# Sums of x1 for the values emitted right behind the transposes of x1, ahead of the tanh products of the new pair

## The chip, the cores and the metric

The kernel runs on one core of one Trainium2 chip. The metric is the device time of one execution in microseconds (us). All data are float32, and all matrix products run in float32 on TensorE (PE in the profile). The other engines are VectorE (DVE), ScalarE (ACT), GpSimd (POOL) and SyncE (SP), whose queue issues all of the DMAs that the text speaks of.

## The reference, cut to what matters

Two graph-attention layers follow each other on x of shape (128, 64, 768), each with a residual and a layer norm. The change lies in the stage that computes layer 0 and the values of layer 1.

```python
# layer 0 (12 heads of 64 features)
h    = einsum('bnd,ade->bane', x, W)
th   = tanh(h)
attn = leaky_relu(th @ w_src + swapaxes(th @ w_dst, 2, 3), 0.2)
attn = softmax(where(~adj, -999.0, attn))
feat = elu(attn @ h + b)                  # heads side by side
gate = sigmoid(x @ H_w.T + H_b)
x1   = layernorm(x + gate * feat + (1 - gate) * x)
# layer 1 (6 heads of 128 features)
q, k, v = x1 @ Wq, x1 @ Wk, x1 @ Wv       # biases left out here
out  = layernorm(x1 + softmax(mask(q @ k.T / sqrt(128))) @ v @ Wf + bf)
```

## The kernel before, in words

The 8192 token rows are 64 tiles of 128 rows; two tiles are a pair, so there are 32 pairs. For each pair three products of 256 rows by a 768x768 weight are computed in the first stage (up to about 1530 us of the profile): `h` (the heads), `g` (the gate) and `v` (the values of layer 1, from x1). Each is done in the manner of Strassen and Winograd with seven block products instead of eight, numbered 1 to 7, so `v6` is block product 6 of the values. The operands are sums of blocks. For `v` they are four sums of blocks of x1 transposed (tile `x1T`, written by ScalarE from PE transposes, 768 features by 256 tokens), made on VectorE by `block_sums` into tiles `sv1` to `sv4` (in the profile all are `sv_v`):

```python
        steps = [
            lambda: e.tensor_tensor(s1, a21, a22, ALU.add),        # L240
            lambda: e.tensor_tensor(s2, s1, a11, ALU.subtract),    # L241
            lambda: e2.tensor_tensor(s3, a11, a21, ALU.subtract),  # L242
            lambda: e2.tensor_tensor(s4, a12, s2, ALU.subtract),   # L243
        ]
```

Blocks a11 and a12 are columns of the pair's first tile (called t0 here), a21 and a22 of its second tile (t1). So s1 needs only the transposes of t1, s2 those of both. Products v6, v5, v7 and v3 read s2, s1, s3 and s4.

The stage is a loop over turns p. Turn p computes `h` and `g` for the new pair p, finishes layer 0 of the old pair q = p - 1, and begins its `v`. The order is written out by hand; no scheduler changes it. A list (`TURN`, for turns 2 to 31 of the new pair; `FIRST`, `SECOND` and `LAST` at the ends) gives the block products in order:

```python
TURN = [
    "h1", "h2", "u4", "u3", "h6", "g1", "h5", "h7", "g2", "g6", "h4",
    "h3", "g5", "g7", "v1", "v2", "g4", "v6", "g3", "v5", "v7",
]
```

(`u` is the value product of the turn before.) `step` issues a product on PE and then the PSUM eviction of the product before it. Behind each step come the actions that `was(pos, ...)` (old pair) and `at(pos, new, ...)` (new pair) have put at that position, in the order in which the calls stand in the code. Each engine works through its instructions in that order. `SECOND_OLD` and `LAST_AT` map positions for the second and the last turn.

Names that the prediction uses, for one turn:

- `by_features` at 8 (t1) and 11 (t0): six PE transposes `x1Tp` (L966) and two ScalarE copies (L967) per tile.
- `products` at 11 (n1, the second tile of the new pair) and 12 (n0, the first): ScalarE's tanh of `h` (L888), VectorE's product with the destination weights (L889), GpSimd's product with the source weights (L890).
- `terms` at 13 (n1) and 14 (n0): VectorE's reduction `sd` of both products (L897), a DMA of it to DRAM (`dstd`, L899), and two DMAs that read it back broadcast over the partitions (`dd`, L902).
- `with_bias` at 13 and 14: GpSimd's addition (L913) and two DMAs `hx` (L918, L919).
- `logits` at 16 (n1) and 18 (n0): VectorE's sum of `dd` and `sd` into `att` (L926). Then `leaky` (ScalarE, L936), `masked` (VectorE, L942 to L949), `exps` (ScalarE, L955, writes `prob`).
- In the next turn: the transposes `pTp` of `prob` (L966), the head products `av` (L987), VectorE's `rden` and `fo` (`features`, L1003, L1004), which read `av` from PSUM and free its banks for the next `pTp`; `gate_tanh` on ScalarE (L1067, L1068).
- `x_sums` at 17: the four sums of the next pair's x, on GpSimd (also L240 to L243). In many turns GpSimd also adds blocks of later weights (`wacc`, L366).

VectorE's eviction of `h` is L851, of the gate L866 to L868, of `v` L880.

Of the kernel before, what the change touches and what calls it, by code (L numbers as in the profile page):

```python
# [59 lines left out]
]  # L60
SECOND_AT = {11: 10, 12: 13, 13: 13, 14: 14, 15: 14, 16: 15, 17: 16, 18: 18, 19: 19, 20: 20}
SECOND_OLD = {
    7.5: 12, 0: 7, 1: 7, 2: 8, 3: 9, 4: 10, 5: 11, 6: 12, 7: 12, 8: 13, 9: 14, 11: 15, 12: 15, 15: 16, 16: 17, 19: 19,
}


# [29 lines left out]
    + [f"q{n}" for n in (0, 1, 2, 3, 4, 5, 6, 8, 7, 9, 10, 11, 12)]  # L96
    + ["v1", "v2", "v6", "q13", "v5", "v7", "q14", "v4", "v3"]
)
LAST_AT = {7.5: 8, 3: 3, 4: 4, 5: 5, 6: 6, 7: 7, 8: 9, 9: 10, 11: 12, 12: 13, 15: 15, 16: 17, 19: 18}


PARTS = ("v", "sp", "sc", "ex", "mult", "split", "send", "turn", "join", "cp", "ctx")
# [32 lines left out]
def kernel(  # L135
# [620 lines left out]
    with ExitStack() as ph, ExitStack() as ph_r:  # L756
# [349 lines left out]
        v_sums, carried = {}, {}  # L1106
        summing = sum_weights(sb)
        for p in range(NP + 1):
            q = p - 1
# [6 lines left out]

            turn, of_new, of_old = TURNS.get(p, (TURN, {}, {})) if new else (LAST, {}, LAST_AT)

            def at(pos, ok, *acts, places=of_new):
                if ok:  # L1120
                    plan.setdefault(places.get(pos, int(pos)), []).extend(acts)

            def was(pos, *acts):
                at(pos, old, *acts, places=of_old)

            def do(f, *args):
                return lambda: f(*args)
# [15 lines left out]
            was(7.5, do(gated, t0))  # L1143
            was(8, do(by_features, t1), do(stats, t0))
            was(9, do(normed, t0))
            was(12, do(v_begins))
            was(15, lambda: v_sums[q][0](), lambda: v_sums[q][1](), do(spill_features, q))
            was(16, lambda: v_sums[q][2]())
            was(19, lambda: v_sums[q][3]())

# [4 lines left out]
            at(8, new, do(inputs, p))  # L1155
            at(11, new, do(products, n1))
            was(11, do(by_features, t0))
            at(12, new, do(products, n0))
            at(13, new, do(terms, n1), do(with_bias, n1))
            at(14, new, do(terms, n0), do(with_bias, n0))  # L1160
# [199 lines left out]
```

## Time and profile before

| what | us |
|---|---|
| median of 3 runs (lowest, highest) | 2900.05 (2900.02, 2900.45) |
| the profiled execution, its own time | 2898.46 |
| span of its trace, first to last instruction | 2896.7 |
| PE busy in the span | 2844.1 |
| VectorE busy | 1936.7 |
| GpSimd busy | 1289.3 |
| ScalarE busy | 1061.6 |
| one turn of the stage, where it repeats evenly | 45.61 |

The profile's page gives busy time by engine, the waits view sums for each pair (who waited, for whom) the idle time in us, the number of times and the longest, and the timeline lists instructions by their start in us, their duration in us, engine, line, operation and tiles; in brackets stands the idle time of the engine before it and what ended it. PE's weight loads are listed as an engine of their own, PEld. Between 60 and 1540 us VectorE is busy 1191.07 us of 1480, PE 1457.04.

### The profile page before, as it was taken

The page shows a single profiled execution, that of the slowest core. Times are in us where ns is not written, and L with a number is a line of the kernel's source. Part 1 is how long each engine was busy: PE and PEld are TensorE (multiplying, and loading weights), DVE is VectorE, ACT ScalarE, POOL GpSimd, SP SyncE. Part 2 cuts the span into 40 slices and gives each one's busy share as a digit, 9 for nine tenths or more (in the row PEclk, how much of TensorE's full clock was granted, in tenths as well). Part 3 has the DMA queues.
Part 4 walks back from the last instruction along what each step waited for, and adds up shares of the span by engine and source line. Part 5 has one row for each costly group of instructions (what it writes and reads, how often), then busy time and mean ns, then how long its engine had stood idle before and what let it go on. Part 6 is the DMA issues. An engine that isn't in the chain of part 4 may idle for free.

```text
span 2896.7 us, 47873 instructions
## 1 busy us (share of the span) xinstructions
PE 2844.1 (98%) x18252; PEld 2074.9 (72%) x18252; DVE 1936.7 (67%) x3203; ACT 1061.6 (37%) x1896; POOL 1289.3 (45%) x1253
## 2 busy tenths in 40 slices
PE   7899999999999999999999999999999999999998
PEld 4566556665566655666668888888888888888886
DVE  6888788888878888887874545555545555554556
ACT  2444444444444444444443123333213333322332
POOL 2434454444535444333443454444545443444534
PEclk9999999999999999999999999999999999999999
DMA  5344444544444444333353434432324333223332
GB/s 176 116 154 154 149 136 150 159 142 149 144 154 147 141 141 139 120 122 104 119 203 83 124 101 110 107 91 75 86 82 111 110 101 93 70 84 95 110 88 74
DMA packets 322068, 348.73 MB, mean 120 GB/s; under 512 B 147888, under 2 KB 247216, under 8 KB 321840
## 3 DMA queue, kind: packets, MB, share of 16 engines
q1 hardware_dynamic: 321840, 345.66, 39.1%
q8 instruction: 146, 2.39, 0.4%
q14 instruction: 82, 0.67, 0.1%
HBM read 198.48 MB, written 122.29 MB: 111 GB/s over the span
## 4 chain that ended last, share of the span: by engine, by line
PE 84%; DVE 8%; DMA 3%; ACT 2%; issue 1%; POOL 1%; SPq 1%; POOLq 0%; DVEq 0%; ACTq 0%
PE z_o L494 8%; PE z_k L447 8%; PE z_q L447 8%; PE y_h L270 7%; PE y_v L270 6%; PE y_g L270 6%; PE y_k L447 6%; PE y_o L494 6%; PE y_q L447 5%; PE z_h L270 4%; PE z_v L270 3%; PE z_g L270 3%; PE x_g L270 2%; PE sp L550 2%; PE cp L634 2%; PE x_h L270 2%
## 5 line engine op out<-in xcount | busy, mean ns | idle before, releaser
L574 ACT ACTIVATE sc<-sc 128x512 f32<-128x512 f32 x48 | 30.7, 639 | 615.0 <-DVE sc L571 615.0
L695 POOL TENSOR_TENSOR y<-y,bf_bc 128x768 f32<-128x768 f32 x64 | 114.7, 1815 | 288.3 <-DMA y<-x1d 288.3
L507 DVE TENSOR_TENSOR y<-y,z_o 128x256 f32<-128x256 f32 x320 | 127.5, 418 | 139.6 <-PE z_o L494 139.4
L494 PE MATMUL z_o<-wf,so 128*128 128x256 f32 x896 | 215.8, 383 | 2.3 <-DVE y L507 1.2
L447 PE MATMUL z_q<-xs,w_wq 128*128 128x256 f32 x896 | 213.5, 381 | 0.3 <-POOL xs L411 0.3
L411 POOL TENSOR_TENSOR so<-ctxT 128x256 f32<-128x256 f32 x224 | 160.1, 731 | 92.3 <-PE y_o L494 47.0
L447 PE MATMUL z_k<-xs,hw_wk 128*128 128x256 f32 x840 | 198.5, 379 | 0.0
L1017 POOL TENSOR_TENSOR x<-gate,x 128x768 f32<-128x768 f32 x64 | 118.2, 1848 | 159.6 <-ACT gate L1068 145.3
L494 PEld LDWEIGHTS z_o<-wf,so 128*128 128x128 f32 x896 | 167.2, 190 | 26.9 <-issue 2.0
L447 PEld LDWEIGHTS z_q<-xs,w_wq 128*128 128x128 f32 x896 | 168.7, 190 | 24.3 <-POOL xs L411 0.7
L322 POOL TENSOR_TENSOR rs_b<-ve_b,minus_half 128x1 f32<-128x1 f32 x64 | 40.5, 632 | 312.9 <-DVE ve_b L320 312.1
L890 POOL TENSOR_TENSOR th<-th,wsd 128x768 f32<-128x768 f32 x64 | 117.3, 1832 | 139.8 <-DVE th L889 139.8
L447 PEld LDWEIGHTS z_k<-xs,hw_wk 128*128 128x128 f32 x840 | 159.5, 190 | 21.7
L322 POOL TENSOR_TENSOR rs_a<-ve_a,minus_half 128x1 f32<-128x1 f32 x64 | 36.0, 562 | 307.8 <-DVE ve_a L320 307.8
L411 POOL TENSOR_TENSOR xs<-r,r 128x512 f32<-128x512 f32 x112 | 147.7, 1336 | 39.3 <-DMA r<-x1Td 22.1
L462 DVE TENSOR_TENSOR qT<-qT,z_q 128x512 f32<-128x512 f32 x96 | 66.0, 688 | 141.7 <-PE z_q L447 141.7
L270 PE MATMUL y_v<-wv,sv_v 128*128 128x384 f32 x384 | 136.4, 491 | 9.3 <-DVE sv_v L241 7.5
L270 PE MATMUL y_h<-w_wq,xT 128*128 128x384 f32 x384 | 136.5, 492 | 8.7 <-DMA w_wq<-in_w_dram 8.1
L462 DVE TENSOR_TENSOR kT<-kT,z_k 128x512 f32<-128x512 f32 x96 | 66.1, 688 | 112.3 <-PE z_k L447 111.2
L270 PE MATMUL y_h<-w_wq,sx_x 128*128 128x384 f32 x384 | 136.5, 492 | 4.2 <-ACT h L850 4.2
L270 PE MATMUL y_g<-hw_wk,sx_x 128*128 128x384 f32 x384 | 136.2, 491 | 2.5 <-DVE hw_wk L219 2.2
L270 PE MATMUL z_v<-wv,sv_v 128*128 128x384 f32 x384 | 137.5, 494 | 1.0 <-DVE v L880 1.0
(165 smaller groups left out, 6913.3 us busy)
## 6 DMA issues: line engine op xcount, KB each, us to landing
x<-in_x_dram SPq DMA_DIRECT2D x64, 384.0 KB, 3.6
dd<-dstd SPq DMA_DIRECT2D x128, 192.0 KB, 3.4
x1d<-x SPq DMA_DIRECT2D x64, 384.0 KB, 2.6
x1Td<-x1T SPq DMA_DIRECT2D x32, 768.0 KB, 4.3
vd<-v SPq DMA_DIRECT2D x64, 384.0 KB, 3.1
r<-x1Td SPq DMA_DIRECT2D x96, 256.0 KB, 3.5
v<-vd SPq DMA_DIRECT2D x384, 64.0 KB, 2.3
y<-x1d SPq DMA_DIRECT2D x64, 384.0 KB, 5.4
```

What stands on the lines that cost most here:

```text
L270: T.matmul(to[:, : self.n], lhsT, rhs, start=kc == 0 and not more, stop=kc == HK - 1, skip_group_check=more,)
L322: G.tensor_tensor(rstd, ve, minus_half, ALU.pow)
L411: G.tensor_tensor(t, self.of(x[0]), self.of(x[2]), x[1])
L447: T.matmul(b[:, half * W2 : (half + 1) * W2], w[:, kc, half * P : (half + 1) * P], x[:, kc, :], start=half == kc == 0 and not more, stop=k ...
L462: V.tensor_tensor(at, at, b.rearrange("p (h t) -> p h t", h=2), ALU.add if sign > 0 else ALU.subtract,)
L494: T.matmul(b[:, :W2], x[:, kc, :], w[:, kc, :], start=kc == 0 and not more, stop=kc == 1, skip_group_check=more,)
L507: V.tensor_tensor(at, at, self.banks[path][:, :W2], ALU.add if sign > 0 else ALU.subtract)
L550: T.matmul(self.sp_[gr * N : (gr + 1) * N, (i * 2 + a) * N : (i * 2 + a + 1) * N], qT[:, 2 * self.f + a, at], kT[:, 2 * self.f + a, at], s ...
L634: T.matmul(self.cp_[a][e, at], self.v_[rows, i, gr, e], self.scT_[rows, at], start=True, stop=True,)
L695: G.tensor_tensor(y, y, pools["bf"], ALU.add)
L890: G.tensor_tensor(th[:, 1, :], th[:, 1, :], wsd[:, 1, :], ALU.mult)
L1017: G.tensor_tensor(xp, st[t]["gate"], xp, ALU.mult)
```

## The change

The sums s1 and s2 leave position 15, where they stood behind both reductions `sd`. s1 goes to position 12, ahead of `products` of n0; s2 goes to position 13, ahead of `terms` of n1. s3 (16), s4 (19) and the DMA of x1T (15) stay. The two maps get an entry for position 13, so that in the second turn both sums stand at the mapped position 15 (ahead of the first `logits` that is evaluated there) and in the last turn at 13 and 14.

```diff
 SECOND_OLD = {
-    7.5: 12, 0: 7, 1: 7, ... 11: 15, 12: 15, 15: 16, 16: 17, 19: 19,
+    7.5: 12, 0: 7, 1: 7, ... 11: 15, 12: 15, 13: 15, 15: 16, 16: 17, 19: 19,
 }
-LAST_AT = {7.5: 8, ... 11: 12, 12: 13, 15: 15, 16: 17, 19: 18}
+LAST_AT = {7.5: 8, ... 11: 12, 12: 13, 13: 14, 15: 15, 16: 17, 19: 18}
...
             was(9, do(normed, t0))
-            was(12, do(v_begins))
-            was(15, lambda: v_sums[q][0](), lambda: v_sums[q][1](), do(spill_features, q))
+            was(15, do(spill_features, q))
             was(16, lambda: v_sums[q][2]())
             was(19, lambda: v_sums[q][3]())
...
             at(11, new, do(products, n1))
             was(11, do(by_features, t0))
+
+            was(12, do(v_begins), lambda: v_sums[q][0]())
+            was(13, lambda: v_sums[q][1]())
             at(12, new, do(products, n0))
             at(13, new, do(terms, n1), do(with_bias, n1))
```

In the built programs the instructions of ScalarE, GpSimd and SP's queue are the same and in the same order before and after; PE's too. On VectorE alone two instructions move in each of the 32 old pairs. In most turns its order from the tanh products on becomes:

```
before: th n1, h3 out, th n0,     sd n1, g out, g out, sd n0, s1, s2, v out, s3, att n1
after:  th n1, h3 out, s1, th n0, s2, sd n1, g out, g out, sd n0,    v out, s3, att n1
```

More of the change, by code (lines that the diff above doesn't have):

```diff
@@ L62 @@
 SECOND_OLD = {
-    7.5: 12, 0: 7, 1: 7, 2: 8, 3: 9, 4: 10, 5: 11, 6: 12, 7: 12, 8: 13, 9: 14, 11: 15, 12: 15, 15: 16, 16: 17, 19: 19,
+    7.5: 12, 0: 7, 1: 7, 2: 8, 3: 9, 4: 10, 5: 11, 6: 12, 7: 12, 8: 13, 9: 14, 11: 15, 12: 15, 13: 15, 15: 16, 16: 17, 19: 19,
 }
@@ L98 @@
 )
-LAST_AT = {7.5: 8, 3: 3, 4: 4, 5: 5, 6: 6, 7: 7, 8: 9, 9: 10, 11: 12, 12: 13, 15: 15, 16: 17, 19: 18}
+LAST_AT = {7.5: 8, 3: 3, 4: 4, 5: 5, 6: 6, 7: 7, 8: 9, 9: 10, 11: 12, 12: 13, 13: 14, 15: 15, 16: 17, 19: 18}
 PARTS = ("v", "sp", "sc", "ex", "mult", "split", "send", "turn", "join", "cp", "ctx")
```

## The prediction

> **What bounds the kernel now.** I read the page first, then the waits, then the timeline of a turn that repeats evenly.
>
> ```profile
> span 2896.7 us, 47873 instructions
> PE 2844.1 (98%) x18252; PEld 2074.9 (72%) x18252; DVE 1936.7 (67%) x3203; ACT 1061.6 (37%) x1896; POOL 1289.3 (45%) x1253
> ```
>
> PE is busy nearly all the time, so only what makes PE wait can cost anything. The waits view of PE and of VectorE:
>
> ```profile
> PE y_v L270 <- DVE sv_v L241: 7.5, 9, 1.4
> ...
> DVE th L889 <- ACT th L888: 97.4, 62, 2.6
> DVE h L851 <- ACT h L850: 74.5, 31, 2.7
> ...
> DVE att L926 <- DMA dd<-dstd: 14.5, 9, 4.6
> ```
>
> The first line is what the change can remove: nine times v6 waits for s2, 7.5 us in all (0.26% of the time). But VectorE is no spare engine here. One turn, timeline:
>
> ```profile
> 1235.40 0.96 DVE L889 TENSOR_TENSOR th<-th,wsd 128x768 f32<-128x768 f32 x1 [2.50 <-ACT th L888]
> ...
> 1236.28 0.55 DVE L851 TENSOR_TENSOR h<-z_h,h 128x384 f32<-128x384 f32 x1
> ...
> 1236.44 1.82 POOL L890 TENSOR_TENSOR th<-th,wsd 128x768 f32<-128x768 f32 x1 [4.25 <-DVE th L889]
> ...
> 1237.91 1.17 DVE L889 TENSOR_TENSOR th<-th,wsd 128x768 f32<-128x768 f32 x1 [1.08 <-ACT th L888]
> ...
> 1239.00 1.74 DVE L897 TENSOR_REDUCE sd<-th 128x24 f32<-128x1536 f32 x1
> 1239.15 1.82 POOL L890 TENSOR_TENSOR th<-th,wsd 128x768 f32<-128x768 f32 x1 [0.89 <-DVE th L889]
> ...
> 1243.37 1.31 DVE L240 TENSOR_TENSOR sv_v<-x1T 128x384 f32<-128x384 f32 x1
> ...
> 1244.71 1.23 DVE L241 TENSOR_TENSOR sv_v<-sv_v,x1T 128x384 f32<-128x384 f32 x1
> ...
> 1246.77 1.31 POOL L242 TENSOR_TENSOR sx_x<-xT 128x384 f32<-128x384 f32 x1
> 1247.14 2.24 DVE L926 TENSOR_TENSOR att<-dd,sd 128x768 f32<-128x768 f32 x1
> ...
> 1261.72 0.56 DVE L851 TENSOR_TENSOR h<-x_h,h 128x384 f32<-128x384 f32 x1 [2.47 <-ACT h L850]
> ...
> 1263.11 0.56 DVE L1004 TENSOR_TENSOR fo<-av,rden 128x384 f32<-128x384 f32 x1
> ...
> 1263.78 0.31 PEld L966 LDWEIGHTS pTp<-ident,prob 128*128 128x128 f32 x3 [0.17 <-issue]
> ```
>
> Follow it back from the end. The second half of `pTp` for t0 begins at 1263.78, 0.11 after `fo` has ended (1263.67): it waits for the bank that `fo` frees. `fo` follows an eviction of h, which waits for ScalarE, which runs exps, two gate_tanh and a copy without a gap, and began when VectorE had masked n0; that follows the second `att`, the first `att`, and back to the tanh products. So a chain of VectorE and ScalarE leads from the transposes x1Tp of t0 through `att` of n1 to `pTp` in the next turn. In the timelines of 31 turns, `fo` to PE's next product (the one behind `pTp`) is 0.50 us in 24, and from that product to the next x1Tp of t0 it is 17.20 us in 30. **A turn is 17.20 + 0.50 + the chain.** Where PE arrives later than `fo`, the first x1Tp to that product takes 28.2 us at least; in most turns it is 28.4 to 30.1. These are about 17 us in all, with the 7.5 us among them, since a PE that waits at v6 would otherwise wait at `pTp`. What matters is therefore when `att` of n1 ends, not v6.
>
> **The Trainium skill.** "SBUF — State Buffer", section "Who interferes with whom", says that a VectorE instruction with two SBUF inputs and a GpSimd instruction that reads SBUF exclude each other for the whole instruction, the first keeping the port, and that tensor_reduce never contends. The trace agrees: L889 takes 0.96 alone and 1.17 above, where it ends 0.81 after POOL's L890 (1238.27), so one that starts second ends at the other's end plus its own time less 0.15; L897 takes 1.74 beside POOL too. "DMA: Bandwidth & Descriptors", section "Anatomy of one DMA — SWDGE (gpsimd) path", puts about 2 us of fixed time on a DMA, mostly completion. It speaks of another path, but these small ones agree: `dstd` lands 1.4 us after issue at least, 2.0 in the median, `dd` 3.4. Two in a row make `sd` to `dd` about 5.7 us, which no engine can shorten.
>
> **The change, step by step**, in the turn above.
>
> 1. Removed: s1 (1.31) and s2 (1.23) between `sd` n0 and `att` n1. VectorE reaches `att` earlier, and v6's wait for s2 goes.
> 2. s1 ahead of th n0. Its inputs are there, so it starts as h is evicted, at 1236.75, inside POOL's L890. By the rule it ends at 1238.27 + 0.55 - 0.15 = 1238.67. Th n0, ready at 1237.88, starts at 1238.60 and now runs alone (0.96), to 1239.56 instead of 1239.08: **+0.48**. The idle 1.08 us hides the rest.
> 3. s2 behind it: it starts before POOL's next L890 can (0.07 after th n0 ends), so it has the port and takes 0.55; successive starts lie 0.08 inside, so **+0.47**. POOL is pushed by 0.7, and `with_bias`, `hx` and x_sums with it; `hx` is needed a turn later.
> 4. `sd` n1 ends 0.95 later (1241.69). Behind it wait the gate's evictions (product g4 needs them 2.1 to 2.9 us later than they now end: covered), `sd` n0 (+0.94) and SP's `dstd`, `dd`. So `dd` of n1, which landed at 1246.43, lands at 1247.38, and `att` starts 0.09 later, 1247.46 instead of 1247.14. VectorE is ready at about 1245.4 and waits 2 us: **the wait for s1 and s2 becomes a wait for `dd`**. Nobody else moves: PE's, ScalarE's, POOL's and SP's order is unchanged.
>
> So the start of `att` n1 shifts by 0.94 + 0.09 - slack, where slack is what `dd` had landed ahead of `att` (0.71 here). I read it for each turn from the landings. Turns by the new pair p:
>
> - Slack 0.02 to 0.62 (p = 3, 4, 5, 6, 8 to 16, 18, 19, 20): shifts of 0.4 to 1.0. E.g. p = 13: `dd` landed 646.56, `att` 646.65, slack 0.09, shift +0.94. Less the room that `fo` has ahead of PE in five of them (up to 0.54) and 0.27 of port time in p = 10: 0.44, 0.40, 0.68, 0.72, 1.0, 0.67, 0.64, 0.21, 0.69, 0.94, 0.50, 0.93, 0.70, 1.0, 0.89, 0.56, sum **+11.0**. In p = 6 and 16 `dstd` waits behind a weight DMA on SP, so I take 0.7.
> - Slack 1.36 to 1.62, v6 had waited and `att` had lasted 2.24 beside POOL's x_sums (p = 2, 7, 17, 21): `att` comes 0.3 to 0.6 earlier, ahead of that L242, and ends 0.9 to 1.2 earlier; the turns give about 1.0, 0.9, 0.9, 1.0, and p = 22 gives 0.3: **-4.1**.
> - The steady turns p = 23 to 30, nearly alike: +0.32 for the start, but `att` meets POOL's L242, now 1247.30 to 1248.29, and ends 1.30 behind it, 1249.6 instead of 1249.38: +0.2 each, **+1.6**. If `att` gets the port first it ends at 1248.98 and PE's floor allows -0.24 each, -2.
> - First old pair: `att` waits 3.0 us for `dd` there, s1 and s2 fit in; v6's 0.62 goes: **-0.6**.
> - p = 31: `att` already waits 4.6 us for `dd` behind the weight loads. A shift of 0 (the loads set it) to 0.95: **+0.5**. Last turn: VectorE has room, 0.
>
> Sum 11.0 - 4.1 + 1.6 - 0.6 + 0.5 = **+8.4 us**. The profiled execution took 2898.46 (its span plus 1.8), so 2906.9; it lies 1.6 below the median of the runs, so against 2900.05 I forecast 2908.4. Bounds: the port rule, 0.8 to 1.0 instead of 0.95 in step 4, 2 us; the steady turns, -3.5 to 0; GpSimd's L366 getting the port ahead of a shifted `att` in some seven turns at 0.6 each, 4 us; landings vary by some tenths. About 2900 to 2918.
>
> **Rivals.** 0.2% is 5.8 us, about what a measurement tells from no change.
>
> - **The wait at v6 goes and nothing takes its place** (faster): 2900.05 - 7.5 = 2892.5. For it: v6 no longer waits for s2, and 1.08 us of VectorE's idle time lies just where s1 goes. Against it: PE stands at `pTp` with no room in most turns. It wins if `dd` doesn't land later, or its slack covers the shift.
> - **s1 finds the port free or `att` wins it**: shift about 0.5 instead of 0.95. The tight turns cost 16 x 0.45 = 7.2 less, 3.8; steady turns -2; with -4.1 and the small ends about 2898: no change.
> - **POOL's second L890 takes the port ahead of s2**: s2 then lasts till POOL's end plus 0.40, some 1.8 us longer, 29 turns, about 52 us more: 2960. Against it: s2 starts 0.15 before POOL can.
>
> **How the numbers follow.** Forecast 0.56 (of it 0.54 slower by over 5.8, 0.02 within), the balanced rival 0.24, v6 alone 0.12, POOL first 0.08. Slower 0.62, within 0.2% 0.26, faster 0.12. The range takes in the forecast's bounds and most of the balanced rival: 2895 to 2920.
>
> **What would show it.** Right: no PE wait for L241; L240 about 1.9 and L889 of n0 back to 0.96; `att` L926 waiting for `dd` in most turns, 14.5 us grown to some 60; more PE waits of `pTp` for `rden` and `fo`. Wrong: steady turns shorter than 45.4 us, or L241 near 2.2 us beside POOL.

## The result and the profile after

| | before | changed |
|---|---|---|
| median of 5 runs each, us | 2900.05 | 2912.57 |
| lowest to highest | 2898.30 to 2900.82 | 2911.70 to 2915.41 |
| profiled execution, its own time | 2898.46 | 2912.57 |
| span of its trace | 2896.7 | 2910.8 |

The ratio is 1.0046, with a 95% interval of 1.0035 to 1.0057: the changed kernel is slower by 12.5 us. In a later set of runs, beside each other on one chip, the medians were 2901.68 and 2915.60, ratio 1.0047 [1.0034, 1.0060].

From the page of the changed kernel, the span, the busy time of the engines and the chain that ended last:

```profile
span 2910.8 us, 47843 instructions
...
PE 2845.7 (98%) x18252; PEld 2074.4 (71%) x18252; DVE 1928.3 (66%) x3203; ACT 1057.6 (36%) x1896; POOL 1296.4 (45%) x1253
...
PE 64%; DVE 17%; DMA 7%; ACT 5%; issue 4%; POOL 2%; SPq 1%; POOLq 0%; DVEq 0%; ACTq 0%
```

The busy times hardly say anything: VectorE even has 8.4 us less to do, and the span is 14.1 longer. The last line does: before, the chain that ended last lay for 84% on PE, 8% on VectorE and 3% on DMA. Now a quarter of it lies on VectorE and DMA. The waits view of VectorE names the place:

```profile
DVE att L926 <- DMA dd<-dstd: 67.5, 36, 4.3
DVE th L889 <- ACT th L888: 67.2, 33, 2.8
```

`att` waits for `dd` 36 times instead of 9, 67.5 us instead of 14.5. The wait of L889 for tanh has shrunk from 97.4 to 67.2 us: s1 now lies in it. And the waits view of PE, first of before:

```profile
PE pTp L966 <- DVE rden L1003: 1.7, 4, 0.9
...
PE pTp L966 <- DVE fo L1004: 1.1, 6, 0.2
```

and of the changed kernel:

```profile
PE pTp L966 <- DVE rden L1003: 16.3, 19, 1.6
...
PE pTp L966 <- DVE fo L1004: 4.7, 27, 0.2
```

No line for L241 is left, which had 7.5 us; PE waits at `pTp` instead, 21.0 us in the two lines, against 2.8 before. The turn p = 26 of the changed kernel, the counterpart of the turn shown of before (there its first line was at 1235.40):

```profile
1247.65 0.96 DVE L889 TENSOR_TENSOR th<-th,wsd 128x768 f32<-128x768 f32 x1 [2.51 <-ACT th L888]
...
1248.53 0.55 DVE L851 TENSOR_TENSOR h<-z_h,h 128x384 f32<-128x384 f32 x1
1248.69 1.82 POOL L890 TENSOR_TENSOR th<-th,wsd 128x768 f32<-128x768 f32 x1 [4.26 <-DVE th L889]
1248.99 1.93 DVE L240 TENSOR_TENSOR sv_v<-x1T 128x384 f32<-128x384 f32 x1
...
1250.84 0.95 DVE L889 TENSOR_TENSOR th<-th,wsd 128x768 f32<-128x768 f32 x1
...
1251.71 0.55 DVE L241 TENSOR_TENSOR sv_v<-sv_v,x1T 128x384 f32<-128x384 f32 x1
1251.87 2.06 POOL L890 TENSOR_TENSOR th<-th,wsd 128x768 f32<-128x768 f32 x1 [1.36 <-DVE th L889]
...
1252.18 1.74 DVE L897 TENSOR_REDUCE sd<-th 128x24 f32<-128x1536 f32 x1
...
1253.95 0.33 SPq L899 DMA_DIRECT2D dstd<-sd  x1
...
1255.40 1.11 SPq L902 DMA_DIRECT2D dd<-dstd  x2
...
1259.67 2.19 DVE L926 TENSOR_TENSOR att<-dd,sd 128x768 f32<-128x768 f32 x1 [2.00 <-DMA dd<-dstd]
```

Read it against the first line of each turn. The reduction L897 started 3.60 us behind it before (1239.00 - 1235.40) and starts 4.53 behind it now. The two DMAs follow at their old distance. VectorE is ready for `att` at 1257.67 and stands idle for 2.00 us, until `dd` has come.

### The profile page after: what moved, and what is told of

Its sections match the earlier page's. It is cut to its first block, busy times and chain, and to the rows that moved or that the text cites. A ratio compares the mean times of both kernels' runs of the same rounds, so it can differ in the third digit from the quotient of the medians.

```text
span 2910.8 us, 47843 instructions
## 1 busy us (share of the span) xinstructions
PE 2845.7 (98%) x18252; PEld 2074.4 (71%) x18252; DVE 1928.3 (66%) x3203; ACT 1057.6 (36%) x1896; POOL 1296.4 (45%) x1253
## 4 chain that ended last, share of the span: by engine, by line
PE 64%; DVE 17%; DMA 7%; ACT 5%; issue 4%; POOL 2%; SPq 1%; POOLq 0%; DVEq 0%; ACTq 0%
PE z_o L494 8%; PE z_k L447 8%; PE z_q L447 8%; PE y_k L447 6%; PE y_o L494 6%; PE y_q L447 5%; PE y_h L270 5%; PE y_g L270 4%; DMA dd<-dstd 3%; DVE att L926 3%; PE z_h L270 2%; DMA dstd<-sd 2%; PE cp L634 2%; PE sp L550 2%; PE x_g L270 2%
## 5 line engine op out<-in xcount | busy, mean ns | idle before, releaser
L890 POOL TENSOR_TENSOR th<-th,wsd 128x768 f32<-128x768 f32 x64 | 125.5, 1960 | 155.5 <-DVE th L889 155.5
L926 DVE TENSOR_TENSOR att<-dd,sd 128x768 f32<-128x768 f32 x64 | 109.7, 1714 | 67.8 <-DMA dd<-dstd 67.5
L270 PE MATMUL z_h<-w_wq,sx_x 128*128 128x384 f32 x384 | 137.6, 495 | 0.7 <-DVE w_wq L216 0.7
```

The costliest lines, as they stand in the source:

```text
L270: T.matmul(to[:, : self.n], lhsT, rhs, start=kc == 0 and not more, stop=kc == HK - 1, skip_group_check=more,)
L890: G.tensor_tensor(th[:, 1, :], th[:, 1, :], wsd[:, 1, :], ALU.mult)
L926: V.tensor_tensor(att3, dd.rearrange("p (m a) -> p a m", a=H0), sd[:, H0:].unsqueeze(2).to_broadcast([P, H0, N]), ALU.add,)
```

## The experiments

Three theories of the 12.5 us were set against each other:

- **D**, the prediction's: `sd` of n1 ends 0.95 us later, `dd` comes later by as much, and the loop VectorE, DMA, `att`, `fo`, `pTp` turns more slowly.
- **P**: it is the port. Sums and products that VectorE and GpSimd stretch against each other cost the time, wherever `sd` stands.
- **V**: what matters is v6's wait for s2. Removing it is a gain, which something unrelated outweighs.

All edits are against the changed kernel, except nodd_before's, which is against before; after_same_chip is the changed kernel itself, best_same_chip is s1_early_s2_behind_sd again. Times are medians, and "before" is the kernel before on the same chip; the two are compared only within one chip.

| kernel | median us | before | ratio, 95% interval |
|---|---|---|---|
| s2_behind_sd | 2896.98 | 2898.29 | 0.9996 [0.9988, 1.0004] |
| s1_early | 2897.72 | 2898.29 | 0.9999 [0.9991, 1.0007] |
| s1_early_s2_behind_sd | 2887.61 | 2898.29 | 0.9965 [0.9951, 0.9978] |
| both_behind_sd | 2899.25 | 2898.29 | 1.0003 [0.9994, 1.0011] |
| spare_ahead | 2909.34 | 2901.19 | 1.0030 [1.0018, 1.0041] |
| spare_behind | 2895.38 | 2901.19 | 0.9981 [0.9974, 0.9987] |
| nodd_before | 2894.57 | 2901.19 | 0.9980 [0.9971, 0.9989] |
| nodd_after | 2881.22 | 2901.19 | 0.9932 [0.9917, 0.9947] |
| s1_early_s2_15 | 2891.65 | 2901.68 | 0.9964 [0.9950, 0.9978] |
| s2_at_14 | 2891.22 | 2901.68 | 0.9960 [0.9947, 0.9973] |
| best_same_chip | 2890.38 | 2901.68 | 0.9960 [0.9946, 0.9974] |
| after_same_chip | 2915.60 | 2901.68 | 1.0047 [1.0034, 1.0060] |

From the timelines of each kernel, three instants of one tight turn (p = 13) and one steady turn (p = 26), in us after the first x1Tp of t0: the end of `sd` n1, the start of `att` n1, and the start of PE's next product behind `pTp`, in the next turn. PE by itself needs 28.18 for the last.

| kernel | 13: sd end | att | product | 26: sd end | att | product |
|---|---|---|---|---|---|---|
| before | 4.99 | 11.11 | 28.50 | 4.99 | 11.39 | 28.42 |
| changed | 5.93 | 11.73 | 29.38 | 5.92 | 11.68 | 28.62 |
| s2_behind_sd | 5.46 | 11.23 | 28.82 | 5.45 | 11.35 | 28.18 |
| s1_early | 5.46 | 11.41 | 28.81 | 5.46 | 11.71 | 28.18 |
| s1_early_s2_behind_sd | 4.98 | 10.55 | 28.18 | 4.99 | 10.87 | 28.18 |
| both_behind_sd | 4.98 | 11.16 | 28.55 | 4.99 | 11.52 | 28.52 |
| spare_ahead | 5.85 | 11.81 | 29.55 | 5.85 | 11.86 | 28.22 |
| spare_behind | 4.99 | 10.84 | 28.46 | 4.98 | 11.21 | 28.21 |
| nodd_before | 4.99 | 11.06 | 28.43 | 4.99 | 11.40 | 28.42 |
| nodd_after | 5.93 | 10.26 | 28.18 | 5.93 | 9.59 | 28.18 |

### One sum at a time: s2_behind_sd and s1_early

The first moves s2 behind the reduction `sd` of n1 and leaves s1; the second moves s1 ahead of the tanh product of n1 and leaves s2.

```diff
 s2_behind_sd:
-            was(13, lambda: v_sums[q][1]())
             at(12, new, do(products, n0))
             at(13, new, do(terms, n1), do(with_bias, n1))
+            was(13, lambda: v_sums[q][1]())
 s1_early:
+            was(11, do(v_begins), lambda: v_sums[q][0]())
             at(11, new, do(products, n1))
             was(11, do(by_features, t0))
...
-            was(12, do(v_begins), lambda: v_sums[q][0]())
```

> The changed kernel with s2 put one place later on VectorE, behind sd of n1 instead of ahead of it; s1 stays ahead of th of n0. Theory D (what costs is that sd of n1 ends later, and so dd of n1 lands later): sd of n1 ends 5.46 us after x1Tp of t0 (before 4.99, after 5.93), half of the loss is gone: about 2905 us, 2901 to 2909. Rival P (the moved sums collide with GpSimd at the SBUF port and push GpSimd's work, dd has nothing to do with it): s2 now runs beside GpSimd's L890 and L913, so the collisions are no fewer: 2911 to 2915.

> The changed kernel with s1 put ahead of th of n1, into VectorE's idle 2.5 us; s2 stays ahead of sd of n1. Theory D: s1 takes 0.55 and costs nothing, th of n0 starts when its tanh is ready, s2 still puts sd of n1 off by 0.47: the other half of the loss is gone, sd of n1 at 5.46, about 2905 us, 2901 to 2909. If the two halves add up, this and the kernel with s2 behind sd together take back what the change cost. Rival P: s1's collision (1.93 us long) was the cost, so nearly all of it is gone: about 2900.

Measured: 2896.98 and 2897.72, within 0.2% of before (2898.29) and below D's range, 2901 to 2909, for either. For s1_early alone P's number, about 2900, lay nearer; for s2_behind_sd P's 2911 to 2915 was 14 us off. The step itself was as D has it: each edit takes `sd` n1 back by half (5.46 instead of 5.93 in both turns of the table), and VectorE's waits of `att` for `dd`, 67.5 us in the changed kernel, fall to these. s2_behind_sd:

```profile
DVE att L926 <- DMA dd<-dstd: 48.3, 35, 4.1
```

s1_early:

```profile
DVE att L926 <- DMA dd<-dstd: 58.3, 35, 5.0
```

What D had wrong is the zero from which it counted. It halved the 12.5 us between before and the changed kernel, as if a kernel without any shift of `sd` were before. But with s1 or s2 moved forward they no longer stand ahead of `att`, and the kernel without a shift, the next one, lies 10.7 us below before; half-way from it to the changed kernel is about 2900. The prediction's own sum for a shift of about 0.5, its balanced rival, had given about 2898.

The other 2 to 3 us lie in part in the tight turns, where PE at its own 28.18 hides the first of a shift, and in part in the steady turns, where the table has PE at 28.18 with either half. There the start of `att` doesn't explain it: in s1_early it is as late as in the changed kernel (11.71 and 11.68). But it lasts 1.56 us, against 2.19 in the changed kernel, where GpSimd's L242 of x_sums starts 0.6 us later after x1Tp (11.57 instead of 10.96), so that most of it runs beside `att`. So in the steady turns P has a part of the cost: GpSimd, pushed back, meets `att` at the port. In the tight turn `att` lasts 1.51 to 1.53 us in every kernel of the table, so there its start decides.

### Both edits: s1_early_s2_behind_sd

s1 ahead of the tanh product of n1, s2 behind `sd` of n1; nothing is left ahead of `sd` that wasn't covered by idle time.

```diff
+            was(11, do(v_begins), lambda: v_sums[q][0]())
             at(11, new, do(products, n1))
             was(11, do(by_features, t0))
-            was(12, do(v_begins), lambda: v_sums[q][0]())
-            was(13, lambda: v_sums[q][1]())
             at(12, new, do(products, n0))
             at(13, new, do(terms, n1), do(with_bias, n1))
+            was(13, lambda: v_sums[q][1]())
```

> Both edits at once: s1 ahead of th of n1, s2 behind sd of n1. Theory D: sd of n1 ends at 4.99 as before and dd lands as before, while s1 and s2 no longer stand between sd of n0 and att of n1 and v6 doesn't wait for s2: faster than the kernel before, att of n1 starts 0.09 behind dd, about 2894 us, 2889 to 2899. Rival P: s2 collides with GpSimd still: 2900 to 2906. Rival V (the wait for s2 at v6 was the only thing to win): 2892.5.

Measured: 2887.61, 10.7 us below before and below all that was expected: 1.4 us under D's range, 5 under V's number, and at least 12 under P's. `sd` n1 is back at 4.98, `att` starts 0.56 earlier than before in the tight turn, and PE comes through at 28.18 in 17 of the 29 turns p = 2 to 30, against 2 of before. Its waits of PE at `pTp`:

```profile
PE pTp L966 <- DVE rden L1003: 4.4, 5, 1.3
...
PE pTp L966 <- DVE fo L1004: 1.6, 9, 0.2
```

6.0 us instead of the changed kernel's 21.0. And the places of s2 and `att` in its timeline, turn p = 26:

```profile
1230.91 0.72 DVE L241 TENSOR_TENSOR sv_v<-sv_v,x1T 128x384 f32<-128x384 f32 x1
...
1236.87 1.52 DVE L926 TENSOR_TENSOR att<-dd,sd 128x768 f32<-128x768 f32 x1 [0.66 <-DMA dd<-dstd]
```

s2 still runs well ahead of v6, so v6 doesn't wait here either. With this as the base, half a shift costs 9.4 us (s2_behind_sd) and 10.1 us (s1_early). Both shifts, the changed kernel, cost 25.2, measured in the last group. P expected the time to follow the port, but s1 has left the port's collision in s1_early (its median in that trace is 0.55 instead of 1.93 us), and s2_behind_sd puts s2 into one (0.72 instead of 0.55); both gain nearly the same, as both bring `sd` back by the same 0.47 us.

### Both sums behind sd: both_behind_sd

```diff
-            was(12, do(v_begins), lambda: v_sums[q][0]())
-            was(13, lambda: v_sums[q][1]())
+            was(12, do(v_begins))
             at(12, new, do(products, n0))
             at(13, new, do(terms, n1), do(with_bias, n1))
+            was(13, lambda: v_sums[q][0](), lambda: v_sums[q][1]())
```

> s1 and s2 both behind sd of n1, ahead of the gate's evictions and of sd of n0. Theory D: sd of n1 at 4.99, dd of n1 as before, sd of n0 up to 2 us later, which dd of n0 has room for in most turns: about 2896 us, 2890 to 2902. Rival P: both sums run beside GpSimd's L890 and L913, as much collision as in the changed kernel: 2908 to 2915.

Measured: 2899.25, inside D's range, but the gain over before that its 2896 stood for isn't there; P's 2908 to 2915 was a miss. `sd` n1 is at 4.98, as D wants it, but `att` starts at 11.16, as in before. Its group of s2 (numbers: least, median and longest ns of one) and its wait of `att`:

```profile
L241 DVE TENSOR_TENSOR sv_v<-sv_v,x1T x32: 962/1928/1936, 90.0 to 1518.1; 128x384 f32<-128x384 f32 x32
```

```profile
DVE att L926 <- DMA dd<-dstd: 14.0, 7, 4.3
```

Behind s1 the sum s2 falls into GpSimd's L913 and lasts 1.93 us. So `dd` is there in time and VectorE comes late, in all but 7 of 64 cases. The port is a real cost here: between `sd` n1 and `att` VectorE has some 1.4 to 2.0 us of room (2.00 idle in the changed kernel; 0.66 idle beside 0.72 of s2 with both edits), and 0.72 + 1.93 us are more than that. `att` waits for the later of two things, `dd` and VectorE; the changed kernel makes the first late, this one the second.

### 0.95 us of reduction ahead of sd, or behind it: spare_ahead and spare_behind

Both are the kernel with both edits and one more reduction per turn, over constants, whose result nobody reads. The only difference between them is its place.

```diff
+        def spare(t):
+            junk = small.tile([P, H0], F32, tag="mx", name=f"spare_{t}")
+            V.tensor_reduce(junk, wsd[:, 0, :].rearrange("p (a e) -> p a e", e=E0), AX.X, ALU.max)
...
 spare_ahead:
+            at(13, new, do(spare, n1), do(terms, n1), do(with_bias, n1))
 spare_behind:
+            at(13, new, do(terms, n1), do(spare, n1), do(with_bias, n1))
```

> The kernel with s1 early and s2 behind sd of n1 (2887.6 us), with a reduction added on VectorE in each turn whose result nobody reads: 128x768, 0.95 us, one input, so no collision with GpSimd; it stands ahead of sd of n1. Theory D: sd of n1 ends at 5.87, as late as in the changed kernel, and though no sum is moved and no port is contended the loss comes back: about 2909 us, 2904 to 2914. Rival P (the port): the reduction takes no port, VectorE has idle time ahead of att: 2888 to 2892.

> The same kernel with the same spare reduction one place later, behind sd of n1. Theory D: dd of n1 is issued as early as without it, VectorE takes the 0.95 us out of its wait for dd: about 2890 us, 2887 to 2896, and so some 15 to 20 us less than with the reduction ahead of sd. Rival P or a plain load of VectorE (0.95 us more work in the chain, wherever it stands): the same time as with the reduction ahead.

Measured: 2909.34 ahead, 2895.38 behind. The same work costs 14.0 us more where it delays `sd` n1, a little less than the 15 to 20 expected. D's sign and nearly its size are shown without any sum of x1 being moved: ahead, `sd` n1 ends at 5.85, close to the changed kernel's 5.93, and the time is 8.2 us above before's. PE's wait at `pTp` in spare_ahead (the lines lie 5 further down in these two kernels):

```profile
PE pTp L971 <- DVE rden L1008: 13.4, 19, 1.4
```

and in spare_behind:

```profile
PE pTp L971 <- DVE rden L1008: 3.0, 5, 0.9
```

VectorE's own wait for `dd` would mislead here: spare_ahead has 38.0 us of it, no more than the 37.8 of the kernel with both edits, since VectorE comes to `att` later by the same amount as `dd`. Such a wait tells how much room VectorE has, not how late `dd` is.

The expectation that no port is contended doesn't hold. The reduction moves s2 into GpSimd's L913, in both kernels alike: the median of L241 is 1.50 us in spare_ahead and 1.51 in spare_behind, against 0.72 without it. So that collision can't make the 14.0 us between them; it may be why spare_behind lies some 5 us above its 2890. The loss of spare_ahead is in the tight turns (29.55 in p = 13). In the steady turn its PE product comes at 28.22, since `att`, though it starts later than in the changed kernel, lasts 1.58 us instead of 2.19.

### Without dd: nodd_before and nodd_after

`logits` adds constants that lie in SBUF instead of `dd`, so that the result is another one; the DMAs are still issued, but nobody waits for them. Once with the order of before, once with that of the changed kernel.

```diff
-                dd.rearrange("p (m a) -> p a m", a=H0),
+                wsd[:, 0, :].rearrange("p (m a) -> p a m", a=H0),
```

> The kernel before, except that logits adds a tile of constants (the weights wsd) to sd in place of dd, so that part of the computation is left out: att waits for no dd, while all of its DMAs are still issued. Theory D: dd bound att in few turns of the kernel before: about 2894 us, 2890 to 2898. Rival P the same.

> The changed kernel with the same replacement of dd in logits (that part of the computation left out). Theory D: without the wait for dd the changed order is the better one, since s1 and s2 no longer stand ahead of att: 2886 us, 2882 to 2891, some 26 us less than the changed kernel and below the kernel before with the same replacement. Rival P: the collisions at the port remain: 8 to 14 us above the kernel before with the same replacement.

Measured: 2894.57 and 2881.22, the second 0.8 us below D's range. Without the wait for `dd`, the changed order is 13.4 us faster than the old one; with it, 12.5 slower. So the later `dd` more than accounts for the whole loss, and hides a gain of 13 us. In nodd_after `sd` n1 ends as late as in the changed kernel (5.93) and s1 stands beside GpSimd as there (median 1.93 us), but `att` starts at 9.59 in the steady turn and PE reaches 28.18 in 25 of 29 turns. So with the collisions kept and the wait for `dd` gone there is no loss but a gain, which P can't explain. The waits of PE in nodd_before:

```profile
PE y_v L270 <- DVE sv_v L241: 8.1, 10, 1.7
...
PE pTp L966 <- DVE rden L1003: 2.2, 2, 2.0
```

and in nodd_after:

```profile
PE pTp L966 <- DVE rden L1003: 2.0, 1, 2.0
...
PE pTp L966 <- DVE fo L1004: 0.5, 3, 0.2
```

In before it isn't `dd` that sets `att`, but VectorE, with s1 and s2 in front of it: nodd_before's turns are those of before (28.43 and 28.42). That it is 6.6 us faster than before has to do with the first old pair, the one place ahead of p = 31 with a long wait for `dd`: up to 95 us PE waits 4.5 us for ScalarE's h and x there, and 9.3 in before, and x1Tp of p = 1 comes at 84.49 instead of 90.19 us. The sixteen turns of the forecast's first group, together, are as long as in before (0.01 us apart). The removal of v6's wait is worth something only where `att` comes earlier as well.

### How much does s2's place matter: the last group

With s1 early, s2 is put at 14, ahead of `terms` of n0 (s2_at_14), and back at its old 15 (s1_early_s2_15); the kernel with both edits and the changed kernel ran beside them. Two map entries for position 14 are not shown.

```diff
+            was(11, do(v_begins), lambda: v_sums[q][0]())
...
 s2_at_14:
+            was(14, lambda: v_sums[q][1]())
 s1_early_s2_15:
+            was(15, lambda: v_sums[q][1](), do(spill_features, q))
```

> s1 ahead of th of n1, s2 back at its old place behind sd of n0. Theory D: dd of n1 as early as in the kernel before, s1 out of the chain, s2 still in it and v6 waiting for it less: some 2 to 5 us over the kernel with s2 behind sd of n1, about 2891 us, 2887 to 2896. Rival P: s1 without collision is all that counts: the same as with s2 behind sd, 2887 to 2889.

> s1 ahead of th of n1, s2 behind the two evictions of the gate, ahead of sd of n0. Theory D: dd of n1 unchanged; s2 now starts 1.1 us later, when GpSimd runs L913, and lasts up to 1.9 instead of 0.7, which VectorE's wait for dd still covers in most turns: 2886 to 2893, about 2889. Rival P: the longer collision costs 1 us a turn: 2905 or more.

> The kernel with s1 ahead of th of n1 and s2 behind sd of n1 once more, so that it, the changed kernel and its neighbours are measured on one chip: 10 to 13 us below the kernel before.

> The changed kernel on the same chip as the three others: 10 to 14 us above the kernel before, 22 to 26 us above the kernel with s1 early and s2 behind sd.

Measured: 2891.65 (at 15), 2891.22 (at 14), 2890.38 (behind `sd` n1), and 2915.60 for the changed kernel. The three lie within 1.3 us and their intervals cover each other. At 15, P too had said the same as behind `sd`, so that run doesn't tell D from P; at 14, P's 2905 or more was a miss, with a median of 1.32 us for s2. So moving s1 is enough for the gain: 0.55 us of work in idle time ahead of a product that waits for tanh, instead of 1.31 us between `sd` n0 and `att`. For s2 each of the three places behind `sd` n1 will do. The best version is 10.7 and 11.3 us faster than before on the two chips, and 25.2 faster than the changed kernel.

## Why the prediction was right, point by point

**The mechanism held, step by step**, in the turn p = 26:

- Step 1, v6's wait for s2: gone.
- Step 2, s1 inside GpSimd's L890: 1248.99 to 1250.92, 1.93 us, where the working has 1.92. This is the exclusion that the Trainium skill states in "SBUF — State Buffer", section "Who interferes with whom". Th n0 ends 3.79 after x1Tp of t0 instead of 3.33, +0.46 (forecast +0.48).
- Step 3, s2 ahead of GpSimd's second L890: it takes 0.55 in this turn; L890 lasts 2.06 instead of 1.82, and so ends 0.24 later for it.
- Step 4, `sd` n1: 5.92 instead of 4.99, +0.93 (forecast +0.95). `att` starts 0.29 later (forecast 0.32) after a wait of 2.00 for `dd` (forecast 2), ends 0.23 later (forecast 0.2), and PE's product comes 0.20 later (forecast 0.2).
- The sign posts: `att` waits 67.5 us for `dd` (forecast some 60), and PE waits longer for `rden` and `fo`.

The spare pair and the nodd pair show the cause from both sides: delay `sd` n1 by other means and the loss is there; take `dd` out of the way and it is not. The port belongs to the same account: s1's collision is what delays `sd` by the first 0.46, and in the steady turns GpSimd's collision with `att` sets when `att` ends (13.63 after x1Tp in before, 13.86 in the changed kernel). But what carries the delay to PE in the tight turns is the wait for `dd`.

**The size was off**: +12.5 by the medians and +14.1 by the profiled spans, against +8.4. The stated range, 2895 to 2920, would have held no change as well, so what tests the forecast is the sum by turns. The changed kernel was profiled twice, the second time in after_same_chip (span 2913.1). Against the one profile of before, each group of turns gives:

| turns | forecast | first profile | second |
|---|---|---|---|
| first old pair | -0.6 | -0.9 | -0.9 |
| sixteen tight turns | +11.0 | +17.3 | +17.5 |
| p = 2, 7, 17, 21, 22 | -4.1 | -2.1 | -2.2 |
| steady, p = 23 to 30 | +1.6 | +2.2 | +1.4 |
| p = 31 | +0.5 | -1.4 | -0.3 |
| sum of the turns | +8.4 | +15.1 | +15.5 |

The rest of the span differences is 1.1 behind the stage in both, and the moment of x1Tp in p = 1: 90.19 in before, 88.07 and 90.03 in the two profiles of one and the same kernel, so that is not the change's doing.

- **Sixteen tight turns: the term that was mis-sized.** It measured +17.3 and +17.5. Three parts of its working fell short. First, `sd` n1 comes later by more than 0.95 where GpSimd's weight sum L366 stands in between, +2.03 in p = 3, +1.18 in p = 14, +1.47 in p = 15, and 2.04, 1.19 and 1.47 in the second profile. Timeline of the changed kernel in p = 3:

```profile
175.18 1.81 POOL L890 TENSOR_TENSOR th<-th,wsd 128x768 f32<-128x768 f32 x1 [3.62 <-DVE th L889]
175.48 1.92 DVE L240 TENSOR_TENSOR sv_v<-x1T 128x384 f32<-128x384 f32 x1
...
176.95 1.04 POOL L366 TENSOR_TENSOR wacc_q<-wacc_q,wadd_q 128x256 f32<-128x256 f32 x1
177.33 1.48 DVE L889 TENSOR_TENSOR th<-th,wsd 128x768 f32<-128x768 f32 x1
```

  L366 gets the port behind s1 and ahead of th n0, which then takes 1.48 instead of 0.96 us. And in p = 14, where it is s2 that stands behind it, with 1.07 instead of 0.55:

```profile
690.17 1.14 POOL L366 TENSOR_TENSOR wacc_k<-wacc_k,wadd_k 128x256 f32<-128x256 f32 x1 [0.73 <-DMA wadd_k<-in_wk_dram]
690.64 1.07 DVE L241 TENSOR_TENSOR sv_v<-sv_v,x1T 128x384 f32<-128x384 f32 x1
```

  The working had L366 as a bound of 4 us ahead of `att`, but not ahead of th n0 and s2, three instructions further up in the same loop. Second, the landing of `dd`: in p = 12 `sd` ends 0.98 and 1.05 later in the two profiles, and `att` starts 1.55 and 0.76 later. And in p = 11 the way from `sd` to the landed `dd` had taken 5.40 in before, the least of the fourteen profiles of all runs, and took 5.93 and 5.90 in the changed kernel. A slack read from one execution is good to some tenths only, and what it lacks goes on to `att`. Third, the way from `att` to `fo` was taken as fixed; in p = 3 it took another 0.36 and 1.10, in p = 13 another 0.25 and 0.35, in p = 15 another 0.31 and 0.66. The timelines show where: in VectorE's instructions with two inputs from SBUF, which meet GpSimd there. In p = 13 of before, L949 of n0 (the last of `masked`) was 0.05 us ahead of L366:

```profile
657.70 0.96 DVE L949 TENSOR_TENSOR att<-att,mx 128x768 f32<-128x768 f32 x1
657.75 1.50 POOL L366 TENSOR_TENSOR wacc_k<-wacc_k,wadd_k 128x256 f32<-128x256 f32 x1 [4.37 <-DMA wadd_k<-in_wk_dram]
```

  In the changed kernel L366 is ahead by 0.34:

```profile
662.25 0.72 POOL L366 TENSOR_TENSOR wacc_k<-wacc_k,wadd_k 128x256 f32<-128x256 f32 x1 [3.99 <-DMA wadd_k<-in_wk_dram]
662.59 1.21 DVE L949 TENSOR_TENSOR att<-att,mx 128x768 f32<-128x768 f32 x1
```

  In p = 3 it is s4 (L243) behind L366, 0.96 and 1.09 instead of 0.57, and in the second profile the `att` of n0, which waits 0.50 for its own `dd`; in p = 15 L949 of n1 lasts 1.76 and 1.70 instead of 1.47 beside x_sums, and in the second profile s4 1.05 instead of 0.54 behind L366. So the first and the third part are in the main one omission: which instructions of VectorE a GpSimd sum gets ahead of when they come later.

  One more 1.7 us, in p = 14 of the first profile, lies outside the loop, between PE's product behind `pTp` and x1Tp (18.89 instead of 17.20); the second profile hasn't it.
- **Five turns that gain.** p = 2, 7, 17 and 21 gave -3.3 and -3.4 (forecast -3.8). p = 22 gave +1.1 and +1.2 instead of -0.3. There `sd` n1 came 2.00 and 1.44 later, not 0.95: a wrong sign from the same omission, th n0 being late.
- **p = 31** became shorter instead of longer. There `dd` waits behind weight loads, and 1.4 and 0.3 less in two executions don't tell how it stands to the change: in the other eleven profiles the turn is between 1.1 shorter and 0.7 longer than before's, in no order with the shift of `sd`.

**The rivals.** V is the rival "nothing takes its place", and fell: the waits at v6 went and PE's waits at `pTp` took their place, larger. The balanced rival, with a shift of about 0.5, is not what the changed kernel did (shift of `sd` 0.93 to 0.94 in both turns of the table); but s2_behind_sd and s1_early are just that case, and they came out at no change, as it said. GpSimd's L890 never got ahead of s2 in the steady turns. That place is taken, if at all, by L366, as in p = 14.

**What stays open** is p = 31, and how much of the excess in the tight turns is L366 and how much the landings of `dd`: no run here took L366 away to price it by itself.

## What to carry to other kernels

Of an engine with idle time, ask which of its instructions starts a long round trip (here a reduction, a DMA out and a DMA back, about 5.7 us): work that is put ahead of that instruction can cost time however idle the engine is (a reduction of 0.95 us there cost 14.0 us more over the run than behind it), and work behind it, or in a wait ahead of it that covers it, can be free. A wait that is removed on the busiest engine is worth only what the loop behind it gives back: the same order that cost 12.5 us with the round trip in the loop gained 13.4 without it. And a move of two instructions is two changes: try them one by one, as here the one sum had its free place four positions earlier, and the other anywhere behind the reduction.

## What the runs showed of the hardware

Where VectorE and GpSimd both have port users queued, the port went from one to the other operation by operation in the turn p = 3 shown above: s1 waited for L890, L366 for s1 (1.04 us), and th n0 for L366 (1.48 us), although th n0's own record begins at 177.33, before s1 ends at 177.40. The turns p = 15 and 22 have the same, in both profiles (L366 1.03 to 1.05 us, th n0 1.47 to 1.48). I had expected an engine that holds the port to keep it for its next instruction where that is ready, as VectorE does from th n0 to s2 in the steady turns (0.55 us), where GpSimd has to wait for th n0 first and is too late. In the first case GpSimd's instruction was already waiting when the port came free, in the second it wasn't.
